# A two-layer state-space and mixture-of-experts kernel: sums over states one to a slot, up to two groups of experts' products to a slot, and quads' last states copied by GpSimdE

## The chip, the cores and the metric

The kernel runs on one core of one Trainium2 chip. The metric is device time in microseconds (us) of one execution; the value given for a kernel is the median of its runs. One more execution is recorded by the hardware profiler, and all durations of single instructions below come from that one. PE is TensorE, PEld its weight loads, DVE is VectorE, ACT ScalarE, POOL GpSimdE, SP SyncE (which issues most DMAs).

## The reference

Input is x of shape (2, 256, 64, 64), read as two batches of 4096 tokens with 256 channels. The computation is, cut to what matters:

```python
x = x + mamba(group_norm(x), L0)           # d_inner 256, 16 states
t = to_tokens(x)
xn = layer_norm(layer_norm(t)) * gamma + beta
t = t + mamba(xn, f) + flip(mamba(flip(xn), b)) + layer_norm(t)   # d_inner 512
t = t + moe(layer_norm(t))
x = from_tokens(t)

# mamba: xz = u @ W_in; xs = silu(causal_conv4(xs)); dbc = xs @ W_x
# dt = softplus(dbc[:16] @ W_dt + b); per channel d and state s, over time:
h = h * exp(dt * A[d, s]) + dt * xs * B[s]
y = sum_s(h * C[s]) + xs * D;   out = (y * silu(z)) @ W_out

# moe, 8 experts: weights w = softmax over experts of mean_over_batches(x) @ Wr + br, per token
h1 = relu(bn1(x @ W1[e]));  h2 = relu(bn2(h1 @ W2[e]));  y_e = h2 @ Wo[e] + bo[e]
out = sum_e w[e] * y_e
```

Since the experts' weights are averaged over the two batches, a token's weights w are known only when both batches are through the scans. The products h1, h2 and h2 @ Wo don't depend on w.

## The kernel before

**Two parts.** The first part (with its own pools) runs all six scans: for each of two batches the layer-0 scan (256 channels), the forward and the backward layer-1 scan (512 channels). Tokens go in 8 chunks of T = 512. The second part, the tail, runs the experts over chunks and both batches, with routing, weighing and the sum.

**Quads and slots.** A tile of 128 rows holds 32 channels times 4 states; four such row groups stand side by side, so a quad is 128 x (4 x 512): 128 channels with 4 states. 128 channels with 16 states are 4 quads. There are 640 quads. Each is done in two halves of 128 x 1024, and a half is a slot: slot = 2g + h, 1280 slots. The loop over quads, `for g in range(nq)`, writes each engine's work slot by slot, and `in_order` fixes that order on every engine. Within eight quads, (n, h) names quad n of the eight and the half h; a layer-0 chunk has 8 quads, a layer-1 chunk 16.

In a slot, in this order: SP's DMAs, pending replica loads; on VectorE the gate of a finished 128 channels (`emit_gate`, L732, at (1,0) and (5,0)); on TensorE the skip product (`emit_skip`), the queue "pe", the sums over states that `SUMS` names for this (n, h), and the queue "pe2" (experts); on ScalarE the copy of the last slot's states (`emit_carry`), two exponentials for the next slot's decay (`emit_decay`, L662, after a join L673), then the queue "act"; on VectorE the queue "dve0", the scan (`emit_scan`, L683), the queue "dve" and, for five quads of eight, the product with C (`emit_times_c`, L692); on GpSimdE the work that `POOL_AT` names, then the queue "pool". The quads 0, 2 and 5 of each eight (`POOL_C`) get their product with C from GpSimdE instead (`emit_times_c_quad`, L708), one quad later (c0 at n = 1, c2 at n = 3, c5 at n = 6), as a whole quad in place. GpSimdE also makes every quad's input dt x B (`emit_b`, L652), three quads ahead, into six buffers bq.

`emit_sum` (L713) adds a quad's four states into a PSUM tile y by four products with a 128 x 32 stack of identities. `emit_gate` then reads y on VectorE.

**States.** A quad's last column is the next chunk's start (`h_state`). ScalarE copies it: per half from PSUM where VectorE multiplies by C (L702), and after the second half from bq for the quads of `POOL_C` (L704). GpSimdE's in-place product with C waits for that last copy.

**Preparation** of a later chunk (`prepare`, `norm`) is put into the same slots by offsets, `SLOTS`. `gate(j)` makes silu of z: products in slot s ("pe"), tanh in s + 1 ("act"), and sz on VectorE in s + 2, in the queue "dve0", ahead of the scan (L541). `norm` for the forward layer-1 scan goes over mean, centre, square, variance, roots, divide and, on GpSimdE, `add`, to `affine` on ScalarE, which overwrites what `add` reads.

**Experts beside the scans.** Once a chunk of the backward scan has left its layer norm (`features`), `experts` plans pairs: a pair is one (batch, chunk, expert). It is 6 groups, layers l = 0, 1, 2 with two halves m each, of two products of 128 x 128 by 128 x 512, followed by a ScalarE eviction in the next slot. The planner goes over the slots, keeps a count `behind` of TensorE's products over `PE_ROOM` = 3.8 a slot and of ScalarE's work, checks that the three PSUM buffers of `psp` suffice (`fits`), and puts at most one group in a slot. `follows` gives the first slot in which a layer's next group may stand. Finished results u go to DRAM. The plan has 67 pairs: all eight chunks of batch 0 and three experts of chunk 7 of batch 1.

**The tail.** `pairs` are the 61 that are left. Each runs two layers (L1189, ReLU on ScalarE L1193), VectorE weighs the result (L1200) and the last layer accumulates in PSUM two pairs later (L1208). Between the pairs stands side work, `side[i]`, a list of steps handed out evenly over the pairs of chunk i: the routing of the next chunk (`routes`: load, norm, sum of batches, logits, spread, which sends the weights over DRAM to all partitions, two buffers wb), and `sums(i)`: load x, add the bias, and for every early result load u, weigh it (L1159) and add it (L1160). `rest` holds the chunks with pairs left, `whole` those without; before, `whole` is empty.

Of the kernel before, what the change touches and what calls it, by code (L numbers as in the profile page):

```python
# [49 lines left out]
KC = C // P  # L50
T = 512
# [8 lines left out]

POOL_C = (0, 2, 5)

SUMS = {(0, 0): (-1,), (2, 0): (0, 1), (4, 0): (2, 3), (5, 1): (4,), (7, 0): (5, 6)}
POOL_AT = {0: "b3", 1: "c0 b4", 2: "b5", 3: "c2 b6", 4: "b7", 5: "b8", 6: "c5 b9", 7: "b10"}
HUGE = 1e37

# [14 lines left out]
PE_ROOM, PE_BEHIND = 3.8, 2.5  # L81
ACT_ROOM, ACT_BEHIND = 2.6, 1.2
# [47 lines left out]
def hybrid_kernel(ctx: ExitStack, tc: tile.TileContext, a: dict, out: bass.AP):  # L130
    nc = tc.nc
# [52 lines left out]
    with ExitStack() as st:  # L184
# [30 lines left out]
        sl = Slots()  # L215
# [98 lines left out]
        def norm(i):  # L314
# [79 lines left out]
            for d, queue, fn in (  # L394
                (-48, "sp", load_x), (-44, "pe", mean), (-43, "dve", centre), (-42, "act", square),
                (-41, "pe", variance), (-40, "act", roots), (-39, "dve", divide), (-39, "pool", add),
                (-38, "act", affine), (-36, "sp", store),
            ):

                sl.put(s0 + d + (6 if c == 0 else 0), queue, fn)  # L400
# [2 lines left out]
            sl.count(s0 - 43, 0, 1)  # L403
            sl.count(s0 - 41, 2, 4, (2,))
            sl.count(s0 - 40, 0, 0, (1,))
            sl.count(s0 - 39, 0, 2)

        def in_proj(job, ck, half, j, name):
            ps = psp.tile([P, T], F32, tag="ps", name=name)
# [8 lines left out]
        def prepare(i):  # L418

            (job, c), ck, tag, s0 = steps[i], cks[i], tags[i], starts[i]  # L420
            nj, at = job.nj, SLOTS[job.nj]
# [106 lines left out]
            def gate(j):  # L528

                v = {}  # L530

                def pe():
                    v["ps"] = in_proj(job, ck, 1, j, f"z_{tag}_{j}")

                def act():
                    v["th"] = wk.tile([P, T], F32, tag="th", name=f"thz_{tag}_{j}", bufs=3)
                    nc.scalar.activation(v["th"], v["ps"], AF.Tanh, scale=0.5)

                def dve():
                    ck["sz", j] = wk.tile([P, T], F32, tag="sz", name=f"sz_{tag}_{j}", bufs=8)  # L540
                    nc.vector.scalar_tensor_tensor(  # L541
                        ck["sz", j], v["th"], 1.0, v["ps"], ALU.add, ALU.mult
                    )

                return (0, "pe", pe), (1, "act", act), (2, "dve0", dve)

            def put(slot, work):
                for d, queue, fn in work:
# [5 lines left out]
            for j in range(nj):  # L554
                put(at["xs"][j], xs(j))
                sl.count(s0 + at["xs"][j], 2, 1, (1,))
                put(at["dt"][j], softplus(j))
                sl.count(s0 + at["dt"][j], 1, 3, (2,))
                sl.count(s0 + at["z"][j], 2, 1, (1,))
            for jp in range(nj // 2):  # L560
                put(at["conv"][jp], conv(jp))
                sl.count(s0 + at["conv"][jp], 5, 1, (1, 2))
# [16 lines left out]
        def at(g):  # L579

            i, jp, n = quads[g]
            return i, 2 * jp + n // SG, n % SG
# [62 lines left out]
        def over_groups(t):  # L645
            return t.rearrange("p (o t) -> p o t", o=1).to_broadcast([P, SG, T])
# [50 lines left out]
        def emit_carry(g, h):  # L697

            i, j, sg = at(g)
            d, two = da.pop((g, h)), slice(2 * h, 2 * h + 2)  # L700
            if quads[g][2] not in POOL_C:
                nc.scalar.copy(steps[i][0].h[:, j, sg, two], d[:, :, T - 1])  # L702
            elif h:
                nc.scalar.copy(steps[i][0].h[:, j, sg, :], bq[g][:, :, T - 1])  # L704

        def emit_times_c_quad(g):
            i, j, sg = at(g)
            nc.gpsimd.tensor_tensor(bq[g], bq[g], over_groups(cks[i]["bc", 1, sg]), ALU.mult)  # L708

        def emit_sum(g):  # L710
# [126 lines left out]
        def experts():  # L837

            last = 2 * nq - 6
            banks = sorted(sl.banks, key=lambda r: r[0])  # L840

            def fits(slot):

                at = sum(b[0] <= slot for b in banks)
                both = banks[:at] + [(slot, slot + 1, 0)] + banks[at:]
                return all(
                    both[k - 3][1] + both[k][2] <= both[k][0] for k in range(max(3, at - 2), min(len(both), at + 4))
                    if at in range(k - 3, k + 1)
                )

            def sums_in(slot):
                n, h = divmod(slot % 16, 2)
                return 1.25 * len(SUMS.get((n, h), ())) + (1 if (n, h) in ((1, 1), (5, 1)) else 0)

            todo = [(at, b, c, e) for at, b, c in sorted(ready) for e in range(E)]
            behind = act_behind = 0.0
            times = [[], [], []]

            def follows(l):

                k, m = divmod(len(times[l]), KC)
                if k == len(todo):
                    return None
                waits = [(l - 1, k * KC + 1, 2)] if l else []
                if m:
                    waits.append((l, k * KC, 1))
                elif k:

                    waits.append((l, k * KC - 1, 6 if l == 0 and todo[k][-1] == 0 else 5))
                    if l < 2:  # L870
                        waits.append((l + 1, k * KC - 1, 0))
                if any(n >= len(times[w]) for w, n, _ in waits):
                    return None
                return max([todo[k][0] + 3] + [times[w][n] + d for w, n, d in waits])

            for slot in range(last):
                behind = max(0.0, behind) + sl.products.get(slot, 0) + sums_in(slot) - PE_ROOM
                act_behind = max(0.0, act_behind) + sl.acts.get(slot + 1, 0) - ACT_ROOM
                if behind + 2 > PE_BEHIND or act_behind + 1.3 > ACT_BEHIND or not fits(slot):
                    continue  # L880
                for l in (2, 1, 0):
                    at = follows(l)
                    if at is None or slot < at:
                        continue
                    banks.insert(sum(b[0] <= slot for b in banks), (slot, slot + 1, 0))
                    times[l].append(slot)
                    behind += 2
                    act_behind += 1 if l == 2 else 1.3
                    break
            put = [  # L890
                (*item[1:], [times[l][k * KC + m] for l in range(3) for m in range(KC)])
                for k, item in enumerate(todo) if (k + 1) * KC <= len(times[2])
            ]
            emit_experts(put)
# [155 lines left out]
    with ExitStack() as st:  # L1050
# [171 lines left out]
        side = {i: [] for i in rest}  # L1222
        for at, i in enumerate(rest):
            after = rest[at + 1 : at + 2]
            now = sums(i)
            if at:
                for j in whole[at - 1 : at]:
                    now += sums(j)
            ahead = []
            for j in whole[at : at + 1] + after:  # L1230
                ahead += routes(j)
            every = max(1, len(now) // max(1, len(ahead)))
            work = side[i]
            while now or ahead:
                work += ahead[:1] + now[:every]
                ahead, now = ahead[1:], now[every:]
# [143 lines left out]
```

## Time and profile before

| | us |
|---|---|
| median of 3 runs | 5331.44 |
| lowest, highest | 5330.82, 5335.3 |
| the profiled execution's own time | 5329.55 |
| its span, first to last instruction | 5327.7 |
| VectorE busy | 4647.7 (87%) |
| TensorE busy | 4401.2 (83%) |
| GpSimdE busy | 4271.5 (80%) |
| ScalarE busy | 3707.4 (70%) |

A busy share is an average over the whole span. The kernel has stages with different limits, so the share of each stretch says more, and in a stretch the waits of the engine that is busiest. An instruction group's line names the line of the source, the engine, the operation, what is written from what with the shapes, the count; then busy time and mean duration, the idle time of the engine just before these instructions, and what ended that idle time. A stall of an engine that isn't the bound costs nothing by itself.

### The profile page before, as it was taken

To read this page: it belongs to the slowest core of one execution; us is meant where nothing else is said; L and a number is where in the kernel's file an instruction comes from. 1 tells how busy PE (TensorE), PEld (TensorE's weight loads), DVE (VectorE), ACT (ScalarE), POOL (GpSimd) and SP (SyncE) were. 2 spreads that over 40 slices of the span, in tenths; PEclk is the share of its full clock that TensorE was granted. 3 is DMA by queue.
4 is the path that set the end of the run, shared out by engine and by line. 5 is a ranking of instruction groups with operands and counts; after the bars stand their busy time and mean duration, and the time that the engine had idled before them with its cause. 6 is when DMAs were issued, how large, how long until landed. Compare 5 with 4: busy or idle time off the path is not lost.

```text
span 5327.7 us, 47305 instructions
## 1 busy us (share of the span) xinstructions
PE 4401.2 (83%) x14920; PEld 1499.7 (28%) x14920; DVE 4647.7 (87%) x3117; ACT 3707.4 (70%) x7728; POOL 4271.5 (80%) x1118
## 2 busy tenths in 40 slices
PE   5677767766678898888878888888998988699999
PEld 1122222221122233222222232233332332244444
DVE  6999999999999999999989999999999999554333
ACT  5677676776767777878887777788778877422332
POOL 6898999999998999998989999999999999411010
PEclk8778788888889999999999999899999999899999
DMA  4445433344334554455555444454545444332332
GB/s 172 139 173 180 139 124 134 127 152 147 131 129 156 189 177 160 164 175 181 191 192 178 160 157 155 166 186 163 178 149 184 171 167 159 132 138 103 111 103 75
DMA packets 306860, 821.11 MB, mean 154 GB/s; under 512 B 34664, under 2 KB 96112, under 8 KB 264624
## 3 DMA queue, kind: packets, MB, share of 16 engines
q1 hardware_dynamic: 302896, 792.78, 43.5%
q0 software_dynamic: 3712, 25.30, 1.2%
q8 instruction: 118, 1.93, 0.1%
q14 instruction: 134, 1.10, 0.1%
HBM read 637.48 MB, written 180.49 MB: 154 GB/s over the span
## 4 chain that ended last, share of the span: by engine, by line
DVE 42%; PE 26%; ACT 12%; issue 9%; POOL 5%; DMA 3%; SPq 0%; DVEq 0%; POOLq 0%; ACTq 0%
DVE da L683 21%; DVE bq L692 8%; PE hp L1189 8%; DVE bq L683 8%; ACT da L662 5%; PE y L1208 4%; PE e L903 3%; POOL bq L652 3%; PE y L713 2%; PE conv L450 2%; PE xs L412 2%; PE o L751 2%; DMA rdt<-dtd 1%; DVE sz L541 1%; PE dbc L479 1%
## 5 line engine op out<-in xcount | busy, mean ns | idle before, releaser
L652 POOL TENSOR_TENSOR bq<-rxdt,bc 128x2048 f32<-128x2048 f32 x640 | 2891.9, 4542 | 42.6 <-issue 20.5
L662 ACT ACTIVATE da<-rdt,w_a 128x512 f32<-128x512 f32 x2560 | 1756.4, 686 | 90.2 <-DVE bq L683 43.9
L683 DVE TENSOR_TENSOR_SCAN da<-da,h_state,bq 128x1024 f32<-128x1024 f32 x700 | 1643.9, 2348 | 12.7 <-issue 8.0
L708 POOL TENSOR_TENSOR bq<-bq,bc 128x2048 f32<-128x2048 f32 x240 | 1086.5, 4527 | 300.9 <-ACT h_state L704 279.8
L713 PE MATMUL y<-bq,stack 128*32 128x512 f32 x5120 | 849.7, 678 | 340.0 <-POOL bq L708 207.1
L692 DVE TENSOR_TENSOR bq<-da,bc 128x1024 f32<-128x1024 f32 x800 | 978.4, 1223 | 24.0
L683 DVE TENSOR_TENSOR_SCAN bq<-da,h_state,bq 128x1024 f32<-128x1024 f32 x420 | 965.1, 2334 | 24.2 <-ACT da L662 24.2
L702 ACT COPY h_state<-da 128x2 f32<-128x2 f32 x799 | 125.8, 157 | 794.0 <-DVE bq L692 792.7
L903 PE MATMUL e<-eh,ew 128*128 128x512 f32 x1072 | 539.6, 631 | 55.4 <-ACT eh L914 27.5
L1193 ACT ACTIVATE h<-hp,of,sc 128x512 f32<-128x512 f32 x244 | 189.6, 777 | 391.6 <-PE hp L1189 375.0
L673 ACT ACTIVATE bq<-h_state,bq,a 128x1 f32<-128x1 f32 x1120 | 431.9, 386 | 0.0
L713 PEld LDWEIGHTS y<-bq,stack 128*32 128x32 f32 x5120 | 152.3, 117 | 984.9 <-issue 376.8
L412 PE MATMUL z<-nx,w_in 128*128 128x512 f32 x640 | 337.9, 656 | 69.5 <-DVE sp L511 46.8
L412 PE MATMUL xs<-nx,w_in 128*128 128x512 f32 x640 | 338.2, 663 | 39.4 <-DVE xc L464 30.3
L450 PE MATMUL conv<-xs,w_conv 64*64 64x512 f32 x2560 | 329.6, 623 | 6.5 <-DVE sp L511 3.6
L903 PEld LDWEIGHTS e<-eh,ew 128*128 128x128 f32 x1072 | 196.2, 197 | 398.4 <-issue 231.8
L751 PE MATMUL o<-sz,w_out 128*128 128x512 f32 x640 | 299.7, 608 | 0.0
L903 PE MATMUL e<-en,ew 128*128 128x512 f32 x536 | 261.3, 614 | 26.5 <-DVE fcen L799 13.3
L1200 DVE TENSOR_TENSOR h<-h,wb 128x1024 f32<-128x1024 f32 x61 | 74.3, 1221 | 210.5 <-ACT h L1193 192.4
L1132 POOL DMA_DIRECT2D w_dram<-wts x8 | 4.3, 544 | 315.3 <-ACT wts L1130 315.3
L720 PE MATMUL y<-xc,w_d 128*128 128x512 f32 x320 | 186.6, 667 | 71.3 <-DVE sz L732 71.3
L515 POOL TENSOR_TENSOR xdt<-sp,xc 128x512 f32<-128x512 f32 x160 | 203.2, 1274 | 44.3 <-DVE sp L511 44.3
(138 smaller groups left out, 5446.2 us busy)
## 6 DMA issues: line engine op xcount, KB each, us to landing
rxdt<-xdtd SPq DMA_DIRECT2D x160, 1024.0 KB, 6.3
rdt<-dtd SPq DMA_DIRECT2D x160, 1024.0 KB, 5.9
bc<-bcd SPq DMA_DIRECT2D x384, 256.0 KB, 3.1
dtd<-sp SPq DMA_DIRECT2D x160, 256.0 KB, 3.6
xdtd<-xdt SPq DMA_DIRECT2D x160, 256.0 KB, 2.8
ew<-in_W SPq DMA_DIRECT2D x134, 256.0 KB, 4.1
u<-eu SPq DMA_DIRECT2D x67, 512.0 KB, 3.9
u<-u SPq DMA_DIRECT2D x67, 512.0 KB, 3.6
```

The source lines that it names most:

```text
L412: nc.tensor.matmul(ps, job.w["in", half][:, k, j * P : (j + 1) * P], rhs, start=(k == 0), stop=(k == KC - 1),)
L450: nc.tensor.matmul(v[r][64 * col : 64 * col + 64, :], job.w["conv"][rows, 2 * jp + j, k, :], ck["xs", jp][rows, j, k : k + T] if k < 4 els ...
L652: nc.gpsimd.tensor_tensor(bq[g], ck["rxdt", j], over_groups(ck["bc", 0, sg]), ALU.mult)
L662: nc.scalar.activation(da[g, h][:, k, :], cks[i]["rdt", j][:, q, :], AF.Exp, scale=steps[i][0].w["a"][:, j, q * SG + sg : q * SG + sg + 1],)
L673: nc.scalar.activation(bq[g][:, q, 0:1], job.h[:, j, sg, q : q + 1], AF.Identity, scale=cks[i]["a0", j][:, h, sg : sg + 1], bias=bq[g][:, ...
L683: nc.vector.tensor_tensor_scan(b if quads[g][2] in POOL_C else d, d, b, job.h[:, j, sg, 2 * h : 2 * h + 1] if c else 0.0, ALU.mult, ALU.add,)
L692: nc.vector.tensor_tensor(bq[g][:, two, :], d, cks[i]["bc", 1, sg].rearrange("p (o t) -> p o t", o=1).to_broadcast([P, 2, T]), ALU.mult,)
L708: nc.gpsimd.tensor_tensor(bq[g], bq[g], over_groups(cks[i]["bc", 1, sg]), ALU.mult)
L713: nc.tensor.matmul(y[i, j][q * CG : (q + 1) * CG, :], stack, bq[g][:, q, :], start=False, stop=(sg == SG - 1),)
L751: nc.tensor.matmul(v[m], job.w["out"][:, j, m * P : (m + 1) * P], ck["sz", j], start=False, stop=(j == job.nj - 1),)
L903: nc.tensor.matmul(ps, ew[l][:, k, m * P : (m + 1) * P], key[x][:, k, :], start=(k == 0), stop=(k == KC - 1),)
L1189: nc.tensor.matmul(ps, we[f"W{l + 1}", e][:, k, m * P : (m + 1) * P], x[:, k, :], start=(k == 0), stop=(k == KC - 1),)
```

## The change

Seven edits, all of order or place; what is computed stays.

1. `SUMS`: the sums that stood in twos at (2,0), (4,0) and (7,0) go one to a slot, the second of each one slot later; the sum of the quad before the eight goes from (0,0) to (0,1).
2. The planner may put several groups in one slot: it tries l = 2, 1, 1, 0, 0 in turn, with its limits checked before each instead of once a slot, and the two halves of a layer may share a slot (the wait of one slot between them is now zero). The plan then has 83 pairs: in addition, the rest of chunk 7, all of chunk 6 and three experts of chunk 5 of batch 1. The tail has 45.
3. sz goes from the queue "dve0" to "dve": behind the scan of its slot instead of ahead of it. The planner counts the PSUM buffer of z for two slots.
4. The last states of the quads 0, 2 and 5 are copied by GpSimdE, just ahead of its product with C, instead of by ScalarE.
5. `affine` of the forward layer-1 norm goes one slot later, save in a scan's first chunk.
6. The planner's count of affine's two evictions goes one slot later, too.
7. In the tail, the sums of a finished (`whole`) chunk are put at the front of a chunk's side work and no longer in turns with the routing; chunk i's own sums still go in turns with the routing.

```diff
--- before.py
+++ after.py
@@ -60,7 +60,7 @@
 
 POOL_C = (0, 2, 5)
 
-SUMS = {(0, 0): (-1,), (2, 0): (0, 1), (4, 0): (2, 3), (5, 1): (4,), (7, 0): (5, 6)}
+SUMS = {(0, 1): (-1,), (2, 0): (0,), (2, 1): (1,), (4, 0): (2,), (4, 1): (3,), (5, 1): (4,), (7, 0): (5,), (7, 1): (6,)}
 POOL_AT = {0: "b3", 1: "c0 b4", 2: "b5", 3: "c2 b6", 4: "b7", 5: "b8", 6: "c5 b9", 7: "b10"}
 HUGE = 1e37
 
@@ -394,7 +394,7 @@
             for d, queue, fn in (
                 (-48, "sp", load_x), (-44, "pe", mean), (-43, "dve", centre), (-42, "act", square),
                 (-41, "pe", variance), (-40, "act", roots), (-39, "dve", divide), (-39, "pool", add),
-                (-38, "act", affine), (-36, "sp", store),
+                (-37 if c else -38, "act", affine), (-36, "sp", store),
             ):
 
                 sl.put(s0 + d + (6 if c == 0 else 0), queue, fn)
@@ -403,7 +403,7 @@
             sl.count(s0 - 43, 0, 1)
             sl.count(s0 - 41, 2, 4, (2,))
             sl.count(s0 - 40, 0, 0, (1,))
-            sl.count(s0 - 39, 0, 2)
+            sl.count(s0 - 38, 0, 2)
 
         def in_proj(job, ck, half, j, name):
             ps = psp.tile([P, T], F32, tag="ps", name=name)
@@ -542,7 +542,7 @@
                         ck["sz", j], v["th"], 1.0, v["ps"], ALU.add, ALU.mult
                     )
 
-                return (0, "pe", pe), (1, "act", act), (2, "dve0", dve)
+                return (0, "pe", pe), (1, "act", act), (2, "dve", dve)
 
             def put(slot, work):
                 for d, queue, fn in work:
@@ -556,7 +556,7 @@
                 sl.count(s0 + at["xs"][j], 2, 1, (1,))
                 put(at["dt"][j], softplus(j))
                 sl.count(s0 + at["dt"][j], 1, 3, (2,))
-                sl.count(s0 + at["z"][j], 2, 1, (1,))
+                sl.count(s0 + at["z"][j], 2, 1, (2,))
             for jp in range(nj // 2):
                 put(at["conv"][jp], conv(jp))
                 sl.count(s0 + at["conv"][jp], 5, 1, (1, 2))
@@ -700,11 +700,10 @@
             d, two = da.pop((g, h)), slice(2 * h, 2 * h + 2)
             if quads[g][2] not in POOL_C:
                 nc.scalar.copy(steps[i][0].h[:, j, sg, two], d[:, :, T - 1])
-            elif h:
-                nc.scalar.copy(steps[i][0].h[:, j, sg, :], bq[g][:, :, T - 1])
 
         def emit_times_c_quad(g):
             i, j, sg = at(g)
+            nc.gpsimd.tensor_copy(steps[i][0].h[:, j, sg, :], bq[g][:, :, T - 1])
             nc.gpsimd.tensor_tensor(bq[g], bq[g], over_groups(cks[i]["bc", 1, sg]), ALU.mult)
 
         def emit_sum(g):
@@ -863,7 +862,7 @@
                     return None
                 waits = [(l - 1, k * KC + 1, 2)] if l else []
                 if m:
-                    waits.append((l, k * KC, 1))
+                    waits.append((l, k * KC, 0))
                 elif k:
 
                     waits.append((l, k * KC - 1, 6 if l == 0 and todo[k][-1] == 0 else 5))
@@ -876,17 +875,16 @@
             for slot in range(last):
                 behind = max(0.0, behind) + sl.products.get(slot, 0) + sums_in(slot) - PE_ROOM
                 act_behind = max(0.0, act_behind) + sl.acts.get(slot + 1, 0) - ACT_ROOM
-                if behind + 2 > PE_BEHIND or act_behind + 1.3 > ACT_BEHIND or not fits(slot):
-                    continue
-                for l in (2, 1, 0):
+                for l in (2, 1, 1, 0, 0):
                     at = follows(l)
                     if at is None or slot < at:
                         continue
+                    if behind + 2 > PE_BEHIND or act_behind + 1.3 > ACT_BEHIND or not fits(slot):
+                        break
                     banks.insert(sum(b[0] <= slot for b in banks), (slot, slot + 1, 0))
                     times[l].append(slot)
                     behind += 2
                     act_behind += 1 if l == 2 else 1.3
-                    break
             put = [
                 (*item[1:], [times[l][k * KC + m] for l in range(3) for m in range(KC)])
                 for k, item in enumerate(todo) if (k + 1) * KC <= len(times[2])
@@ -1222,15 +1220,14 @@
         side = {i: [] for i in rest}
         for at, i in enumerate(rest):
             after = rest[at + 1 : at + 2]
-            now = sums(i)
+            now, work = sums(i), side[i]
             if at:
                 for j in whole[at - 1 : at]:
-                    now += sums(j)
+                    work += sums(j)
             ahead = []
             for j in whole[at : at + 1] + after:
                 ahead += routes(j)
             every = max(1, len(now) // max(1, len(ahead)))
-            work = side[i]
             while now or ahead:
                 work += ahead[:1] + now[:every]
                 ahead, now = ahead[1:], now[every:]
```

## The prediction

> **What bounds the kernel now.** I read the busy time by stretch first, cutting the span where the work changes: before the first expert product (about 1600 us), to the last scan (4593 us), the hand-over, and the tail (from the first tail product, 4618 us). Columns: stretch, its length, then busy us and instruction count of PE, PEld, DVE, ACT, POOL, then the TensorE clock, the DMA share and GB/s.
>
> ```profile
> 0.00:1600.00 1600.00, 1113.18 (x4051) 326.94 (x4052) 1496.91 (x997) 1122.99 (x2409) 1436.71 (x371) 0.83 0.42 146
> 1600.00:4593.00 2993.00, 2587.37 (x9184) 870.84 (x9184) 2878.91 (x1867) 2373.16 (x5037) 2754.86 (x692) 0.94 0.49 168
> 4593.00:4618.00 25.00, 11.61 (x24) 4.28 (x21) 0.69 (x1) 1.17 (x2) 1.25 (x2) 0.70 0.38 124
> 4618.00:5328.00 710.00, 689.05 (x1664) 297.69 (x1664) 271.18 (x253) 210.10 (x281) 78.63 (x54) 0.99 0.33 114
> ```
>
> There are two bounds. In the scans VectorE is busy 94% and 96% of the first two stretches; TensorE has 406 us free in the second. In the tail TensorE is busy 97% and VectorE 38%. So a pair moved out of the tail saves TensorE's price of it there; beside the scans it costs only what makes VectorE wait.
>
> Next the groups of instructions, for the prices (busy us, mean ns of one, idle before them and its releasers):
>
> ```profile
> L903 PE MATMUL e<-eh,ew 128*128 128x512 f32 x1072 | 539.6, 631 | 55.4 <-ACT eh L914 27.5 <-DVE fcen L799 16.8 <-DVE sz L541 5.0
> L1189 PE MATMUL hp<-h,W 128*128 128x512 f32 x488 | 235.6, 605 | 0.6
> L1189 PE MATMUL hp<-n,W 128*128 128x512 f32 x488 | 223.2, 600 | 13.4 <-DMA n<-nf_dram 13.4
> L1208 PE MATMUL y<-h,Wo 128*128 128x512 f32 x488 | 221.9, 598 | 6.3 <-DVE h L1200 6.3
> L1160 DVE TENSOR_TENSOR x<-x,u 128x1024 f32<-128x1024 f32 x67 | 94.0, 1403 | 12.0 <-POOL x L1154 9.2
> L1159 DVE TENSOR_TENSOR u<-u,wb 128x1024 f32<-128x1024 f32 x67 | 88.6, 1322 | 34.6 <-DMA u<-u 34.6
> L704 ACT COPY h_state<-bq 128x4 f32<-128x4 f32 x240 | 45.6, 190 | 29.7 <-DVE bq L683 27.2
> ```
>
> The 488 of each tail row are 61 pairs times 8; the 67 of the sums are the pairs done early.
>
> Then the waits of the scan part (total us, times, longest), VectorE's first, then GpSimdE's and TensorE's:
>
> ```profile
> DVE sz L541 <- ACT thz L537: 66.3, 39, 4.1
> DVE xc L464 <- ACT thx L459: 34.6, 14, 15.3
> DVE bq L683 <- ACT da L662: 28.1, 24, 2.2
> DVE sz L732 <- PE y L713: 12.8, 18, 3.0
> ...
> POOL bq L708 <- ACT h_state L704: 279.8, 113, 7.2
> ...
> PE y L713 <- POOL bq L708: 207.1, 78, 11.4
> PE y L713 <- DVE bq L692: 132.1, 102, 3.3
> ```
>
> The largest repairable stall of the binding engine is sz: its tanh comes up to 4.1 us late while a ready scan stands behind it. TensorE's waits on bq cost nothing today; they are room that experts can't use, since TensorE takes its instructions in order.
>
> **What the Trainium skill says.** "TensorE: Matmul & The Clock Gate", Part 1: an idle window of about 3.4 us puts the array to half rate. The trace agrees; the timeline shows the same group of four expert matmuls before and after a 3.98 us gap:
>
> ```profile
> 3709.36 1.98 PE L903 MATMUL e<-eh,ew 128*128 128x512 f32 x4
> ...
> 3715.85 0.14 PEld L713 LDWEIGHTS y<-bq,stack 128*32 128x32 f32 x4 [3.98 <-DVE bq L692]
> ...
> 3717.06 3.41 PE L903 MATMUL e<-eh,ew 128*128 128x512 f32 x4
> ```
>
> The gap ends in a sum waiting for VectorE, just the wait that spreading takes away. The same page's table calls ScalarE, VectorE and GpSimdE strictly first in, first out; the sz stall above is that. "GPSIMD Engine Reference", section 3.1, has 4497 ns for a two-input operation on 2048 fp32; the trace has 4527 (L708). No page prices a 4-element GpSimdE copy.
>
> **The change part by part.** Base: the profiled execution, 5329.55 us, of which the span is 5327.7. It stands 1.9 us below the median of the runs, 5331.44.
>
> *The plan.* Applying the planner's rule in both versions gives 67 pairs before and 83 after. The tail keeps 128 - 83 = 45 instead of 61. Before, no slot has more than one group (one layer, one half: four matmuls); after, 302 slots have one, 96 two, 2 three.
>
> *Tail, saving.* A pair costs TensorE (235.6 + 223.2 + 221.9)/61 = 11.16 us there; 16 of them 178.6 us. Chunks 6 and 7 are now wholly early; routing and bias of all eight chunks stay, and so does the 25 us hand-over, in which the first loads wait for the last store.
>
> *Tail, added.* Sixteen more stored results: 16 x (1.322 + 1.403) = 43.6 us on VectorE, less 16 weighings at 1.22 (L1200) = 19.5. VectorE goes to 295 of about 531 us, 56%: hidden on average. The fullest stretch is chunk 4: 8 pairs, 89 us of TensorE, beside 24 stored results, 65 us, 10 us of weighing and about 2 of routing. That fits narrowly. But chunk 5 now routes two chunks in five pairs, so that the third routing weight tile waits for one of its two buffers until chunk 5's last weighing, and the 7.8 us load (L1134) comes after. Moving the finished chunk's sums ahead releases buffers but makes routing later. The trace shows how such a load looks once: 18.1 us of VectorE idle, 6.3 of TensorE's. None lost to 25 us; I take 10.
>
> *sz behind the scan.* Put after the scan, sz comes 2.35 us later in VectorE's queue (L683), and the waits are 66.3/39 = 1.7 us in the mean. I take 55 of 66 us away (40 to 63): the longest outlast 2.35. Behind a late sz now stand that slot's product with C and the next scan. The bank that z holds longer is booked by the planner.
>
> *States copied by GpSimdE.* ScalarE loses 240 x 0.19 = 46 us. GpSimdE gains 240 small copies in its queue between products. The multiply behind each also waits for the copy's completion, since it overwrites what is read. The nearest rows are its memset of 128x1 (99 ns) and its affine select of 128x128 (292 ns); with the wait I take 0.3 us each (0.1 to 0.6), 72 us in all. It has 280 us of waiting at just this place, and the wait on the copy becomes one on the scan. The product behind c2, which has little wait ahead of it, may be 0.3 us late for its sum at slot (4,0): 80 x 0.3 = 24 us of TensorE's room at most. On the path 0; if the cover were gone, the 72 us would be VectorE's wait for bq.
>
> *Sums spread; affine one slot later.* The same 640 sums. At (0,0), (2,0), (4,0) and (7,0) the last in the list needs a product that VectorE has only just begun; a slot later it is there, and much of the 132 us goes from TensorE. The sum before the gate at (1,0) has one slot of lead instead of two: that row stands at 12.8 us and may grow by some. Affine takes a 16 us wait on GpSimdE's add out of ScalarE's queue. VectorE: 0 (-8 to +5).
>
> *Sixteen pairs beside the scans.* TensorE: 797.6 us of L903 in this stretch over 67 pairs is 11.9 each, 190 in all; 2587 + 190 = 2777 of 2993, 93%. ScalarE: (205.1 + 77.3)/67 = 4.2 each, 67 us; against it some 30 of its 46 us lie here: 79% to 81%. SP: three weight loads and one store each (256 and 512 KB), 20.5 MB more in 3 ms, 7 GB/s on 168. These come beside waiting replica loads on SP's queue; as each replica is asked for slots ahead, 0. What is late next is TensorE's share of what VectorE waits for: in this stretch 15.8 us for da, 7.2 xc, 6.2 y, 5.7 norms, together 35. TensorE's free time falls from 406 to 216 us, by 1.9; waits growing alike give 35 x 0.9 = +31. I take +30. Bounds: nothing (sums that no longer block) to 190 (no cover).
>
> **Sum.** -178.6 + 10 - 55 + 30 = -194 us: 5329.55 - 194 = 5136; with the 1.9 us to the median, 5138.
>
> **Rivals.**
> All hidden: sz nearly gone (-63), no pressure, tail stalls 0: 5329.55 - 63 - 179 = 5088. For it: an extra group costs 1.98 us where TensorE is free 14% of the time, and half-rate stretches shrink. Against: in the chain of waits around 3640 to 3670 us TensorE already carries the end through conv, dbc and o, slots without slack.
>
> TensorE becomes the second stretch's bound: 60% of the 190 us shows (+114): 5329.55 - 55 + 114 - 169 = 5220. For it: 93% is little room for a queue fed by three engines, and its waits for fsq (58 us) and fcen (30 us) stay. Against: much of "busy" is modelled ends and half-rate matmuls.
>
> The tail feeds late: two routings in five pairs and 24 sums in eight stall TensorE for 50 us instead of 10: 5176. For it: VectorE's 75 of 89 us in chunk 4. Against: VectorE is 38% busy now, and TensorE waited for it once, 6.3 us.
>
> Slower than before: the double slots. Two groups take 2 x 1.98 us, and the slot's other products (about 2.2 planner units of about 0.94 us) 2.1: 6.0 us in a slot of 4593/1280 = 3.6. If that 2.4 us, and some psum-buffer queueing (0.4 us), reached VectorE at each of the 98, it would be 98 x 2.8 = 274 us against gains of 224: 5380. It decides above 2.3 us a slot. Against: the planner puts no group where it counts more than 2.5 units behind.
>
> **How the numbers follow.** Forecast 0.54 (its own range 5100 to 5180); all hidden 0.10; tail late 0.10; TensorE the bound 0.18; slower 0.08. The range 5085 to 5220 leaves out about a tenth above with the slower case and under a tenth below. A difference under 0.2% (11 us) could not be told from no change here. Faster by over 0.2%: 0.91; within: 0.01; slower: 0.08.
>
> **What would show it.** Tail: 45 pairs near 11.2 us, last scan to end about 566 us instead of 735. Scan part near 4568 us instead of 4593. The sz row of VectorE's waits under 15 us; TensorE's wait on DVE bq under half of 132; GpSimdE's wait on L704 gone and one on the scan in its place, copies of 0.1 to 0.3 us. TensorE at some 93% in the second stretch. I'm wrong if VectorE's waits for xc, sp or da there grow by over 100 us, or TensorE has over 30 us of waits in the tail.

## The result and the profile after

The changed kernel takes 5347.78 us (median of 8 runs, 5336.98 to 5351.08) against 5331.38 before (8 runs too): a ratio of 1.0026, 95% interval 1.0015 to 1.0037, so it is 0.3% slower. The forecast was 5138. The pairs did leave the tail; the time came back in the scans, and part of it in the tail.

The stretches of the changed kernel, cut at the same events as those of before (last scan, first product of the tail), with the same columns:

```profile
0.00:1600.00 1600.00, 1120.20 (x4028) 323.57 (x4032) 1467.27 (x991) 1107.93 (x2315) 1442.55 (x450) 0.83 0.42 145
1600.00:4723.00 3123.00, 2737.31 (x9592) 914.79 (x9586) 2882.74 (x1873) 2427.18 (x4987) 2796.80 (x853) 0.94 0.49 169
4723.00:4749.00 26.00, 12.92 (x24) 4.74 (x24) 0.69 (x1) 1.17 (x2) 1.25 (x2) 0.70 0.34 116
4749.00:5345.00 596.00, 538.92 (x1280) 234.04 (x1280) 285.62 (x267) 160.10 (x217) 76.84 (x54) 0.94 0.43 150
```

The second stretch is 130 us longer with the same VectorE work in it: VectorE's share falls from 96% to 92%. TensorE's rises only from 86% to 88%, so the engine that got the new work is not full. The tail is 114 us shorter, not 169.

In this document a scan part ends where the last scan starts: 4588.9 us before, 4719.4 after (+130.5). The rest of the span went from 738.8 to 625.5 (-113.3). The sum is the +17.2 us of the profiled spans.

VectorE's waits in the scan part of the changed kernel, total us, times, longest:

```profile
DVE sz L731 <- PE y L712: 212.8, 79, 7.4
DVE xc L464 <- ACT thx L459: 38.3, 16, 14.7
DVE bq L683 <- ACT da L662: 18.1, 16, 2.2
DVE da L683 <- ACT da L662: 18.1, 20, 2.7
```

Each line is called a row below: all the waits of one kind together. The first row is the gate (L732 before): from 12.8 us in the whole span to 214.8. The row of the late tanh (sz from thz, 66.3 us) is down to 2.4. One wait of VectorE was removed and another, three times as large, put in its place.

The timeline of the changed kernel around one gate shows how (start, duration, engine, line, operation, in brackets the idle time before it):

```profile
4028.57 2.34 DVE L683 TENSOR_TENSOR_SCAN bq<-da,h_state,bq 128x1024 f32<-128x1024 f32 x1
...
4030.83 0.67 DVE L541 SCALAR_TENSOR_TENSOR sz<-thz,z 128x512 f32<-128x512 f32 x1
4031.41 2.35 DVE L683 TENSOR_TENSOR_SCAN bq<-da,h_state,bq 128x1024 f32<-128x1024 f32 x1
4031.55 3.70 PE L901 MATMUL e<-en,ew 128*128 128x512 f32 x8 [1.37 <-DVE sz L541]
...
4035.08 1.88 PE L412 MATMUL xs<-nx,w_in 128*128 128x512 f32 x4
...
4036.89 1.07 PE L712 MATMUL y<-bq,stack 128*32 128x512 f32 x8
...
4038.03 0.69 DVE L731 SCALAR_TENSOR_TENSOR sz<-y,sz 128x512 f32<-128x512 f32 x1 [4.28 <-PE y L712]
```

The two scans that write bq belong to quad 0. Its product with C is GpSimdE's, so its slots are the shortest on VectorE, 2.35 us of scan (plus an sz in the first) instead of 3.6. In the same two slots TensorE has two expert groups (3.70 us), then xs (1.88), the next job in its queue, and only then the sum that the gate reads. The two groups themselves began 1.37 us late: they waited for the PSUM buffer that sz gives back, and sz now stands behind its scan. VectorE is at the gate 2.4 us after it began slot (0,1); the scan behind the gate, which needs nothing from it, is held up for 4.28 us.

Lead is the time from a sum's place to the gate that reads it. The change took a slot of lead from two sums, that before the gate at (1,0) and that of quad 3 before the gate at (5,0). Taking the gates of the whole span by the scan that follows (one that writes da follows (1,0), one that writes bq follows (5,0)), of 79 gates at (1,0) 60 wait, 154 us together, and of 80 at (5,0) 19 wait, 58 us. Before it was 5 and 6 us. The slot ahead of (5,0) is quad 4's second, with a product of VectorE in it, and so 1.2 us longer than that ahead of (1,0). Expert groups aren't needed for a late gate: 48 of the gates at (1,0) have no expert product begun in the two slots ahead of them, and they wait 71 of the 154 us.

### The profile page after: what moved, and what is told of

The parts are those of the page before. It is cut to its first block, busy times and chain, and to the rows that moved or that the text cites. A ratio compares the mean times of both kernels' runs of the same rounds, so it can differ in the third digit from the quotient of the medians.

```text
span 5344.9 us, 47471 instructions
## 1 busy us (share of the span) xinstructions
PE 4409.3 (82%) x14920; PEld 1477.1 (28%) x14920; DVE 4636.3 (87%) x3131; ACT 3696.4 (69%) x7520; POOL 4317.4 (81%) x1358
## 4 chain that ended last, share of the span: by engine, by line
DVE 42%; PE 29%; ACT 11%; issue 8%; POOL 5%; DMA 4%; SPq 0%; DVEq 0%; POOLq 0%; ACTq 0%
DVE da L683 21%; DVE bq L692 10%; PE e L901 7%; DVE bq L683 5%; ACT da L662 5%; PE hp L1187 4%; PE y L712 4%; PE conv L450 3%; POOL bq L652 3%; PE xs L412 3%; PE o L750 2%; PE y L1206 2%; POOL bq L707 1%; DMA dtd<-sp 1%; PE dbc L479 1%
## 5 line engine op out<-in xcount | busy, mean ns | idle before, releaser
L652 POOL TENSOR_TENSOR bq<-rxdt,bc 128x2048 f32<-128x2048 f32 x640 | 2891.2, 4539 | 43.4 <-DMA rxdt<-xdtd 16.1
L683 DVE TENSOR_TENSOR_SCAN da<-da,h_state,bq 128x1024 f32<-128x1024 f32 x700 | 1644.2, 2349 | 26.9 <-ACT da L662 18.1
L712 PE MATMUL y<-bq,stack 128*32 128x512 f32 x5120 | 784.6, 661 | 190.2 <-POOL bq L707 140.3
L901 PE MATMUL e<-eh,ew 128*128 128x512 f32 x1328 | 680.6, 642 | 117.4 <-DVE sp L511 40.2
L901 PEld LDWEIGHTS e<-eh,ew 128*128 128x128 f32 x1328 | 242.0, 198 | 550.2 <-issue 229.3
L901 PE MATMUL e<-en,ew 128*128 128x512 f32 x664 | 337.0, 636 | 41.8 <-DVE sz L541 26.2
L1191 ACT ACTIVATE h<-hp,of,sc 128x512 f32<-128x512 f32 x180 | 139.7, 777 | 307.5 <-PE hp L1187 290.3
L712 PEld LDWEIGHTS y<-bq,stack 128*32 128x32 f32 x5120 | 122.6, 113 | 776.8 <-issue 402.5
L706 POOL COPY h_state<-bq 128x4 f32<-128x4 f32 x240 | 45.4, 189 | 313.8 <-DVE bq L683 305.8
L731 DVE SCALAR_TENSOR_TENSOR sz<-y,sz 128x512 f32<-128x512 f32 x160 | 109.7, 686 | 215.9 <-PE y L712 214.8
L499 PE MATMUL dt<-dbc,w_dt 64*128 64x512 f32 x320 | 210.1, 741 | 89.8 <-ACT dbc L486 72.9
```

The source lines that it names most:

```text
L652: nc.gpsimd.tensor_tensor(bq[g], ck["rxdt", j], over_groups(ck["bc", 0, sg]), ALU.mult)
L683: nc.vector.tensor_tensor_scan(b if quads[g][2] in POOL_C else d, d, b, job.h[:, j, sg, 2 * h : 2 * h + 1] if c else 0.0, ALU.mult, ALU.add,)
L712: nc.tensor.matmul(y[i, j][q * CG : (q + 1) * CG, :], stack, bq[g][:, q, :], start=False, stop=(sg == SG - 1),)
L901: nc.tensor.matmul(ps, ew[l][:, k, m * P : (m + 1) * P], key[x][:, k, :], start=(k == 0), stop=(k == KC - 1),)
```

## The experiments

Each is given with its ratio to the kernel before and the 95% interval of that ratio. The dense plan is the changed kernel's, with two or three groups in some slots; the sparse plan has one at most.

**e1.** Only the two sums that feed a gate go back; the planner still counts the sums where the change has them (`PLANNED`), so that all pairs keep their slots.

```diff
-SUMS = {(0, 1): (-1,), (2, 0): (0,), (2, 1): (1,), (4, 0): (2,), (4, 1): (3,), ...}
+PLANNED = {(0, 1): (-1,), ..., (4, 0): (2,), (4, 1): (3,), ...}
+SUMS = {(0, 0): (-1,), (2, 0): (0,), (2, 1): (1,), (4, 0): (2, 3), ...}
```

> The changed kernel, with only the two sums that feed a gate put back two slots ahead of it: the sum of quad -1 at (0,0), that of quad 3 at (4,0); the other sums stay one to a slot, and the planner still counts the sums where the changed kernel has them, so that the 83 pairs stand in the same slots. Theory A (lead): VectorE's 215 us of waiting for y at the gate comes from the last sum standing one slot ahead of it; the row falls under 25 us and the kernel to 5135 to 5185 us. Theory B (density): TensorE is late because of the 16 added pairs and double groups, wherever the sums stand; the row keeps over 120 us, the time stays above 5270.

Measured 5216.58 us, ratio 0.9787 (0.9772 to 0.9802): 131 us less than the changed kernel. The scan part ends at 4591.6, 128 us earlier. VectorE's wait at the gate, in the whole span:

```profile
DVE sz L732 <- PE y L713: 60.7, 34, 4.0
```

Neither theory's ranges were met, but lead is the larger part: it is worth 154 of the 202 us. With the old lead and the new plan the row is still 61, not 13.

**e2.** The reverse: the kernel before with the same two sums one slot ahead, its plan kept (again by `PLANNED`).

> The kernel before, with only the same two sums moved to one slot ahead of the gate ((0,1) and (4,1)); plan of 67 pairs in the same slots, sz ahead of the scan, ScalarE's copies. Theory A: VectorE's wait for y at the gate grows from 13 to 150 to 250 us, and the kernel is 100 to 200 us slower, 5430 to 5530. Theory B: without the added pairs TensorE is in time, the row stays under 60 us and the kernel within 40 us of 5331.

5372.85 us, ratio 1.0081 (1.0066 to 1.0096), 42 us slower than before: between the two expectations, just above that of theory B. The gate's row:

```profile
DVE sz L733 <- PE y L714: 72.1, 50, 4.9
```

So the late sum costs here a third of the 131 us that e1 shows. That isn't yet the share of the plan, since e2 lacks the small edits too (sz behind its scan, GpSimdE's copies, affine, the other sums spread); e3 and g4 below have them.

**e3.** The changed kernel with the old planning rule.

```diff
-                for l in (2, 1, 1, 0, 0):
+                for l in (2, 1, 0):
...
+                    break
```

> The changed kernel with the planner's old rule, at most one group to a slot and a slot between the halves of a layer (66 pairs planned); all else as changed. Theory A: VectorE's wait at the gate stays above 130 us; the scan part stays within 60 us of the changed kernel's, the tail is 17 pairs longer (about 190 us less its repaired stalls), so 5400 to 5500 us. Theory B: the wait at the gate falls under 60 us, the scan part by 150 us, and the time is 5320 to 5380.

5374.99 us, ratio 1.0088 (1.0071 to 1.0105), a time that theory B named. But the gate waits 129 us, just under what theory A said, and the scan part ends at 4624.0, 95 us before the changed kernel's, between the two theories (60 and 150).

**g4.** The missing corner with both repaired: e1 with the old planning rule.

> As e1, with the old rule of one group to a slot (66 pairs). The difference in the scan part to e1 is the price of the 17 added pairs beside the scans. If they cost VectorE little, the scan part is within 20 us of e1's and the kernel about 110 us slower (tail): 5310 to 5340. If their price is what eats the gain, the scan part is 50 to 90 us shorter than e1's: 5240 to 5290.

5270.29 us, ratio 0.9887 (0.9872 to 0.9902). Its scan part ends at 4522.3, 69.3 us before e1's. That is the price of the 17 further pairs beside the scans, and the second theory's. They pay all the same: e1 is 54 us faster, by the tail.

The gate's rows of e3 and then g4:

```profile
DVE sz L731 <- PE y L712: 129.3, 69, 7.0
DVE sz L732 <- PE y L713: 28.5, 21, 3.1
```

Now four kernels differ in lead and plan alone. The gate's row is 28.5 us (two slots, sparse: g4), 61 (two slots, dense: e1), 129 (one slot, sparse: e3) and 215 (one slot, dense: the changed kernel). In scan part the late sums cost 101.7 us in the sparse plan and 127.8 in the dense one, so the plan adds only 26 us to their price. The larger step is from e2 to e3: with the sparse plan in both, the late sums cost 41 us of scan part in the kernel before and 102 beside the small edits. Which of these edits does it wasn't tried apart.

**g1 and h1.** Two other ways to give the gate lead, both with the sums in the changed kernel's slots: the gate behind its slot's scan (g1), or the sum ahead of its slot's other products on TensorE (h1).

```diff
-                if (n, h) in ((1, 0), (5, 0)) and done:
-                    emit_gate(*done.pop(0))
...
                 emit_scan(g, h)
+                if (n, h) in ((1, 0), (5, 0)) and done:
+                    emit_gate(*done.pop(0))
```

> The changed kernel with the gate of (1,0) and (5,0) placed behind that slot's scan on VectorE instead of ahead of it; the sums stay where the change put them. If lead is what is short, the scan of 2.35 us gives more of it: with 80 waits of 2.7 us in the mean, VectorE's wait at the gate falls from 215 to about 60 us, and the kernel to 5210 to 5260 us. If TensorE is simply behind (density), the wait moves behind the scan but stays above 150 us, and the time above 5290.

```diff
+                first = (n, h) in ((0, 1), (4, 1))
+                if not first:
+                    sl.run(slot, "pe")
                 for m in SUMS.get((n, h), ()):
...
+                if first:
+                    sl.run(slot, "pe")
```

> The changed kernel with the two gate sums still in slots (0,1) and (4,1), but ahead of that slot's other products on TensorE instead of behind them. If what is late is the queue of products ahead of the sum in its own slot, VectorE's wait at the gate falls from 215 us to 60 to 120 and the kernel to 5220 to 5280 us. If TensorE is already behind when it enters the slot, the wait stays above 150 us and the time above 5290.

g1: 5247.2 us, ratio 0.9841 (0.9827 to 0.9856), the gate's row 61 us. h1: 5249.86 us, 0.9848 (0.9833 to 0.9863), the gate's row 110 us, both rows in the scan part. Both fit the first theory of their expectation, and both fall short of e1. In g1 the wait for xc rises to 82 us (38 in the changed kernel), and TensorE's skip product waits 178 us for the gate instead of 76; convolutions, which xc needs, stand behind it on TensorE.

**g2 and x1.** What sz behind the scan is worth: taken back in e1 (g2), done alone in the kernel before (x1).

```diff
-                return (0, "pe", pe), (1, "act", act), (2, "dve", dve)
+                return (0, "pe", pe), (1, "act", act), (2, "dve0", dve)
```

> As e1 (gate sums two slots ahead), with sz back ahead of its slot's scan. If sz behind the scan is worth what the row said, VectorE waits again 55 to 90 us for its tanh and the kernel is 35 to 80 us slower than e1's 5217: 5250 to 5295. If the wait only moved to later instructions (da, xc, y), it is within 20 us of e1.

> The kernel before with sz behind its slot's scan, nothing else. If a stall's row is what it is worth, 40 to 63 us faster than before (5331): 5270 to 5290. If the wait only moves on (the product with C and the next scan then stand behind sz, and ScalarE is the late one in any case), within 15 us of before: 5316 to 5346.

g2: 5223.62 us, ratio 0.9796 (0.9782 to 0.9811), 7 us above e1 with overlapping runs; its gate's row is 40 us against e1's 61, so with sz ahead of the scan the gates wait less. x1: 5322.44 us, 0.9982 (0.9973 to 0.999), 9 us faster than before. The waits of VectorE in the scan part of x1:

```profile
DVE xc L464 <- ACT thx L459: 43.9, 18, 15.5
DVE da L683 <- ACT da L662: 43.3, 34, 2.7
DVE sz L732 <- PE y L713: 35.3, 27, 5.2
```

The 66 us row is gone (2.4 left), and da rose by 40 us, the gate by 22, xc by 9: 72 us in three other rows. So VectorE meets ScalarE and TensorE a little later instead; that the wait on the tanh had let them catch up is my reading. Part of the gate's rise fits the buffer that sz holds for longer: TensorE's waits on sz before z, xs and expert products rise from 20 us to 55.

**g3 and x2.** The copies of the last states: given back to ScalarE in e1 (g3), given to GpSimdE in the kernel before (x2).

```diff
-            elif h:
-                nc.scalar.copy(steps[i][0].h[:, j, sg, :], bq[g][:, :, T - 1])
...
+            nc.gpsimd.tensor_copy(steps[i][0].h[:, j, sg, :], bq[g][:, :, T - 1])
```

> As e1, with the last states of quads 0, 2 and 5 copied by ScalarE again, as before the change. If GpSimdE's copies are free (45 us of busy time in 280 us of waits), the time is within 10 us of e1's 5217; if they pay by taking work from ScalarE's full queue, it is 10 to 30 us slower; if they cost by holding products back, 10 to 30 us faster.

> The kernel before with the states of quads 0, 2 and 5 copied by GpSimdE, nothing else. From g3, where they were worth 21 us beside 83 pairs: 10 to 30 us faster than before, if what they relieve is ScalarE's queue; if they matter only beside the denser plan, within 8 us.

g3: 5238.26 us, ratio 0.9823 (0.9807 to 0.984), 22 us above e1. x2: 5295.85 us, 0.9934 (0.9917 to 0.995), 36 us faster than before, more than I had allowed. The copies take GpSimdE 45.4 us in the changed kernel (189 ns each, as on ScalarE), in waits that it had. What the two differences are made of shows with x4.

**x4.** A single operation stands out in the timeline of the kernel before. VectorE, then GpSimdE, 135 to 155 us:

```profile
136.39 18.12 DVE L827 TENSOR_TENSOR sc<-sc,bn 128x32 f32<-128x32 f32 x1
154.44 0.18 DVE L828 TENSOR_TENSOR of<-bn 128x32 f32<-128x32 f32 x1
```

```profile
134.11 4.56 POOL L652 TENSOR_TENSOR bq<-rxdt,bc 128x2048 f32<-128x2048 f32 x1
138.60 2.51 POOL L515 TENSOR_TENSOR xdt<-sp,xc 128x512 f32<-128x512 f32 x2
141.04 4.52 POOL L708 TENSOR_TENSOR bq<-bq,bc 128x2048 f32<-128x2048 f32 x1
145.49 8.97 POOL L652 TENSOR_TENSOR bq<-rxdt,bc 128x2048 f32<-128x2048 f32 x2
```

An operation of 128x32 lasts 18.1 us, until GpSimdE's unbroken run of products ends (154.46); its like takes 0.18. In x2 it takes 2.9 us and ends at 140.04, just as one GpSimdE product hands over to the next:

```profile
137.10 2.94 DVE L826 TENSOR_TENSOR sc<-sc,bn 128x32 f32<-128x32 f32 x1
139.96 2.48 POOL L515 TENSOR_TENSOR xdt<-sp,xc 128x512 f32<-128x512 f32 x2
```

x4 moves this operation and its three neighbours to GpSimdE, in the kernel before.

```diff
-                nc.vector.tensor_tensor(sc, sc, bn[:, :, M_G], ALU.mult)
+                nc.gpsimd.tensor_tensor(sc, sc, bn[:, :, M_G], ALU.mult)
...
```

> The kernel before with four operations of 128x32 that stand once in the program (the experts' scales and offsets, L827 to L830) on GpSimdE instead of VectorE. If the first of them, 18.1 us in the profile, is held by GpSimdE's products and holds VectorE's queue, the kernel is 12 to 19 us faster than before's 5331 and VectorE has no such operation; then 15 of the 36 us of x2 are this one stall, and the rest is ScalarE's queue. If the 18 us are a wait that VectorE would have had in any case, within 5 us.

5315.54 us, ratio 0.997 (0.9959 to 0.9982): 16 us, as the first theory had it. So some 15 of the 36 us of x2 are this one stall. The other 20 I put down to ScalarE's shorter queue: two rows of VectorE's waits for ScalarE fall by 18 us in x2 (sz from 66.3 to 52.7, bq from 28.1 to 24.0). No run has that part alone.

The same stall is back in g3 (its duration in ns stands there three times, since the operation stands once):

```profile
L828 DVE TENSOR_TENSOR sc<-sc,bn x1: 18399/18399/18399, 135.6 to 135.6; 128x32 f32<-128x32 f32 x1
```

In e1 it takes 2.85 us. g3's scan part is only 14.0 us longer than e1's; this stall is enough to account for it, and the other 6 us lie in the tail, where nothing was changed. So beside the dense plan the copies as such are worth nothing that these runs can show.

**x3.** The other two sums (quads 1 and 6) a slot later, alone, in the kernel before.

> The kernel before with only the sums of quads 1 and 6 one slot later ((2,1) and (7,1)); the gate sums stay two ahead, the plan stays. If TensorE's waits on products just begun, and the half-rate stretches behind them, delay what VectorE waits for, 20 to 50 us faster than before; if they cost nothing, as the forecast had it, within 10 us.

5331.35 us, ratio 1.0 (0.9991 to 1.0008): nothing.

**e4, b3, b1, h2: the tail, and a version that beats both.** In the tail of the changed kernel SP's queue reads (start, time over which the instructions were issued, how many):

```profile
4839.13 0.39 SPq L1161 DMA_DIRECT2D out<-x  x1
4839.57 1.86 SPq L1156 DMA_DIRECT2D u<-u  x3
...
4846.94 12.98 SPq L1156 DMA_DIRECT2D u<-u  x4
4870.80 0.39 SPq L1161 DMA_DIRECT2D out<-x  x1
```

A finished chunk's store (`out<-x`) waits for VectorE's last sum of it, and the loads of the next early results (`u<-u`) stand behind it; VectorE then idles until they land (64.8 us, 12 times). e4 is e1 with the store issued after up to three further early results.

```diff
         def store(b, i):
+            held.append((b, i))
+
+        def put_out(b, i):
             nc.sync.dma_start(
...
             nc.vector.tensor_tensor(x[b, i], x[b, i], u, ALU.add)
+            since[0] += 1
+            if held and since[0] % 3 == 0:
+                put_out(*held.pop(0))
```

> As e1, and in the tail the store of a finished chunk is issued by SP only after up to three further early results have been loaded, instead of at once, where it waits in SP's queue for VectorE's last sum with the next loads behind it. If the store standing ahead of the loads is what starves VectorE in the tail, its wait for u (65 us) falls under 30 us and the kernel is 15 to 40 us faster than e1. If instead the two buffers of routing weights or the three of u are, it is within 10 us of e1.

5194.28 us, ratio 0.9747 (0.9732 to 0.9761), 22 us below e1, with VectorE's wait for u at 11.7 us. b3 adds buffers (three of wb, five of u):

> As e4, and in the tail three buffers of routing weights instead of two and five of early results instead of three. If the routing weights' wait (28 us of VectorE, 20 of GpSimdE) delays TensorE, the kernel is 8 to 20 us faster than e4's 5194: 5174 to 5186. If the tail's rest is the first loads and the routing chain, it is within 6 us.

5200.13 us, 0.9751 (0.9737 to 0.9766): no gain. The theory that the two routing buffers hold the tail falls. b1 is e4 with the gate behind the scan:

> As e4 (gate sums two slots ahead, late store), with the gate also behind its slot's scan. If the 59 us that VectorE still waits at the gate in e4 is only short lead, it goes under 15 us and the kernel is 20 to 50 us faster than e4's 5194. If the skip product behind the gate then holds TensorE's convolutions, as the wait for xc in g1 (82 us against 45) suggests, the gain is eaten: within 15 us of e4 or slower.

5196.11 us, 0.9745 (0.9729 to 0.9761), level with e4. The gate's row falls from 59 us to 3, and what it held shows elsewhere: the wait for xc goes from 46.9 us in e4 to 73.7, that of the scans writing bq for ScalarE from 36.5 to 47.8, and that of scans for GpSimdE's state copy from 4.1 to 22.7.

h2, with h1's sums and b3's tail:

> As h1, with the late store and the buffers of b3 in the tail. If scan part and tail add up, it is faster than h1 by what b3 is faster than e1's 5217, 25 to 45 us; if the sums at the head of their slot are better than two slots ahead, it is the fastest of all, under b3.

5229.08 us, 0.9812 (0.9797 to 0.9826): 21 us faster than h1, under the 25 to 45 expected, and the scans stay behind e1's. e4 and b1 are the fastest measured, 2.5% below before.

## Why the prediction was wrong

The step that failed is in "Sums spread; affine one slot later": "The sum before the gate at (1,0) has one slot of lead instead of two: that row stands at 12.8 us and may grow by some", costed at 0 (-8 to +5). The mechanism was named and mis-sized, and the second sum that lost its slot, before the gate at (5,0), wasn't named. The row grew by 202 us, and e1 shows what the lost lead is worth in time: 128 us of scan part, 131 us of the median. I counted the lead in slots, of 3.6 us in the mean. In VectorE's time the slot before (1,0) is 2.35 us, because quad 0 has no product with C there, while TensorE's queue before the sum was made longer and later by the same change. The prediction's own list of signs names VectorE's waits for xc, sp and da, and not the gate.

The miss of 210 us splits well. In the scan part the forecast was -25 and the runs show +130.5, 155 us more: 128 for the two sums and 39 for the pairs, less 12 because the small edits together gave 67 us and not 55. The other 55 us lie in the tail.

*Sixteen pairs beside the scans, +30.* e1 against g4 has 69 us for 17 pairs. The kind of cost was right, VectorE's waits growing, and mis-sized: from g4 to e1 the gate's row grows by 32 us, and the waits of the scans for ScalarE's da, of which I had counted the TensorE share alone, by 30. The bounds (0 to 190) held it.

*Tail, added, 10.* The tail fell by 114 us, not 169. TensorE's busy time fell by 150 (689 to 539), not 179, and its idle time rose from 21 to 57 us, past the 30 that the prediction had named as a sign of being wrong. The groups of the changed kernel:

```profile
L1187 PE MATMUL hp<-h,W 128*128 128x512 f32 x360 | 173.6, 606 | 2.2 <-ACT h L1191 1.7
L1187 PE MATMUL hp<-n,W 128*128 128x512 f32 x360 | 172.4, 624 | 13.7 <-DMA Wo<-in_Wo 13.7
L1206 PE MATMUL y<-h,Wo 128*128 128x512 f32 x360 | 171.1, 621 | 26.3 <-DVE h L1198 26.3
L1157 DVE TENSOR_TENSOR u<-u,wb 128x1024 f32<-128x1024 f32 x83 | 108.7, 1309 | 64.8 <-DMA u<-u 64.8
```

A pair now costs 517.1/45 = 11.49 us instead of 11.16: the products of the first and the last layer take 624 and 621 ns against 600 and 598, in a stretch whose granted clock is 0.94 against 0.99. Why it is lower wasn't tried. I had looked for the stall at the routing buffers; b3 says they aren't it. SP's queue, whose order I didn't follow through the tail, is a part: 22 of the 55 us come back in e4. The rest, with the first loads and two routings in five pairs among the candidates, is open.

*sz, -55.* x1 has -9, g2 makes it -7. The row did go, as forecast, but the next late engine stood right behind it. The prediction said what stands behind a late sz, but not what ScalarE and TensorE would do with 66 us less time. It took the longer use of z's buffer as settled by the planner's count; TensorE waited for it all the same.

*States copied by GpSimdE, 0.* x2 has -36 us. The price of a copy was 0.19 us, within the bounds. Some 15 of the 36 are the one stall of 18 us, which the prediction didn't price and which goes away with this edit by luck. About 20 are left in the kernel before, and nothing beside the dense plan (g3).

*Other sums spread, 0.* x3 has 0.0. Right.

By the scan part: before to g4 -66.6 (the small edits, of which x1 gives -8.5 and x2 -34.9 alone, the stall of 18 us included; affine's, one pair fewer and their interplay aren't separated), g4 to e1 +69.3, e1 to the changed kernel +127.8; together +130.5. Of the rivals, "Slower than before: the double slots" came nearest in time (5380), but for another reason: it put 2.8 us of loss at each of 98 slots, and the loss sits at the gates, by lead more than by groups. "TensorE becomes the second stretch's bound" has TensorE full; it is 88% busy there, late at one place.

*The pause in the timeline.* The 3.98 us that the prediction sets beside the 3.4 us of the page is the pause of the weight loads. The products themselves paused for 3.07 us there (L713, begun at 3715.86 us). So that place shows the same group at 1.98 us before a pause and at 3.41 after it, but it doesn't confirm the length of 3.4 us. No term of the sum rested on it.

## What to carry to other kernels

Count the lead between a producer and an in-order consumer in the consumer's own time at that place, not in slots: it can be shortest just where an engine's work was taken away. If the consumer stands at the head of a queue of independent work, being late there holds all of it, so give such sums their lead before adding work ahead of them.

A row of waits isn't what its repair wins. Here it won less each time: 66 us of sz gave 9, 154 us of the gate gave 131, 53 us of the loads in the tail gave 22. So ask which other engine used that pause to catch up.

Price an edit by itself as soon as several are made together, and look for single instructions of odd length before giving a difference to the edit's purpose: here one operation of 18 us was 15 of the 36 us that 240 copies seemed to win in the kernel before, and about all of their worth beside the dense plan.

## What the runs showed of the hardware that was not expected

An operation of VectorE with both operands in SBUF was held for 18 us by GpSimdE's unbroken products (L827, above), and its removal is worth 16 us (x4). The Trainium skill, "SBUF — State Buffer", section "SBUF: two separate sides", says that such an operation and a GpSimdE operation that reads SBUF take one shared pair of ports as an exclusive lock, for a whole instruction. The trace agrees that one blocks the other, and adds that the wait can be far longer than one instruction. In the kernel before, VectorE's operation was passed over at five changes from one GpSimdE instruction to the next and ended with the last of them. In all five kernels in which ScalarE makes the copies and the operation is VectorE's (before, e2, x1, x3, g3) it lasts 16.1 to 18.6 us. In the twelve with GpSimdE's copies no operation of these four lasts over 4.5 us, and in x2 the first of them got its turn at such a change, with no gap in GpSimdE's work. Why the same place goes one way or the other isn't shown. The scans and products with C, which take one operand from PSUM, keep to 2.35 and 1.22 us beside the same products.
